# Context products on all 128 rows, bulk loads from ScalarE's queue, key scaling on GpSimd, one score bank per head

## The chip, the core and the metric

The kernel runs on one core of a Trainium2 chip. The core's engines run side by side and wait for each other by semaphores: TensorE (PE, with its weight loads shown apart as PEld), VectorE (DVE), ScalarE (ACT), GpSimd (POOL) and SyncE (SP), which here does nothing but issue DMAs. All DMAs run on the core's 16 DMA engines. The metric is device time of one execution, in microseconds (us).

## The reference, cut to what matters

The input is 4 sequences of 1024 tokens with 512 features. After a layer norm, an attention block and a small rounded product are added to the input. The attention has 16 heads of 128 features and two branches. The sparse branch attends to pooled entries (one for every four tokens, 256 a sequence), of which each query keeps the best 8. The local branch attends to a band of 128 tokens back. The two contexts are averaged and projected:

```python
q = apply_rope(rmsnorm(q, qn_w), pos)                       # 16 heads
ck = apply_rope(rmsnorm(entries @ Wk + bk, kn_w), block_ends)  # pooled keys, shared by the heads
cv = entries @ Wv + bv
sc = jnp.where(causal, einsum(q, ck) * scale, NEG)
tv, ti = jax.lax.top_k(sc, TOPK)                            # softmax over the best 8
lk = apply_rope(rmsnorm(hidden @ Wlk + blk, kn_w), pos)     # local keys, 16 heads
sl = jnp.where(band mask, q . lk * scale, NEG)              # 256 columns: last and this chunk
merged = (ctx_sparse + ctx_local) * 0.5
out = merged @ Wo + bo
```

`rmsnorm` divides by the root of the mean square and multiplies by a weight of the feature. `apply_rope` turns the first 64 features in pairs by an angle of the position: `x1*cos - x2*sin` and `x1*sin + x2*cos`.

## The kernel before

**Units and steps.** Tokens are cut into 32 chunks of 128, the heads into 8 pairs. One chunk with one pair of heads is a unit; there are 256. A step `s` of the main loop issues the scores of unit `s` and, in an order written out by hand, parts of the units around it: projections of unit `s+3`, normalization and rotation of `s+2`, values of `s+1`, context product of `s-1`, output projection of `s-2`. There is no scheduler's choice in it: each engine runs its instructions in the order of the text, and waits by semaphores where data or buffers are not ready.

**Chunks.** `c` is a chunk's place in its sequence, 0 to 7. It sets `m = 32 (c+1)`, the number of pooled entries that the unit's queries may see. The first 32 units (four chunks) run chunk by chunk. From unit `FIRST` = 32 on, units come in pairs of an even and an odd chunk, so `c` alternates (0, 1, 0, 1, ... for 16 units, then 2, 3, and so on), and the query and key projections of a pair are made together in seven products instead of eight, from combined weights: four blocks of 256 KB for each pair of heads, computed once by GpSimd, kept in DRAM and loaded again for each pair of chunks.

**The way of a unit.** `scores` (L964, L971, L974) writes both heads' scores to one PSUM tile of two banks. `weigh` adds masks and finds maxima on DVE (L995, L1009, L1016, L1017) and marks the best 8 (L1019); ACT then takes exponentials (L1021, L1029). `settle` on DVE drops what is not among the best 8 and takes the reciprocal of the sums (L1037, L1048); `divide` on ACT multiplies by it (L1055). `turn` transposes 32x32 blocks on DVE (L1073) and stores the result to DRAM (`pr<-probB`, L1081); `fetch` reads it back in four pieces with the blocks exchanged (`probT<-pr`, L1122), which makes a full transpose. `values` multiplies by the values (L1139) in the next step: for each head the last chunk's and this chunk's local values and one or two blocks of pooled values. Each such fp32 product appears as two MATMUL records. `keep_context` (L1155, ACT) and `to_output` (L1170, PE) end the unit.

**Queries and keys.** After the projection, ACT sums squares (`squares`, L413) and GpSimd makes the factor of each row and head (`spread`, L407 and L408). In the next step `normalize` multiplies on DVE by factor and weight, four instructions of 128x128 (L842), and `rotate` does the turn by angles: one product on GpSimd (L429), one on DVE (L431), sum and difference on GpSimd (L434, L435). `turn_keys` transposes blocks on DVE (L896, L899) and stores them (`qk<-thb`, L905, four DMAs); `fetch_keys` reads them back (L915, two).

**Queues.** From the first unit on, SyncE issues every load and store, in the order of the text. In a step of the pairs that order is: two of the pair's four loads of combined weights (`load_combined`, L352, 256 KB each, a ring of six places), `pr`, four `qk`, four `probT`, `qT` and `lkT`, stores of a chunk in preparation, and in every second step a load of output weights (`load_wo`, L169, 512 KB). Every DMA signals one of eight completion counters, taken in turn along the list of all DMAs, and in the built program a DMA waits at its issue until the DMA eight places before it has landed, unless that is known already. Across a step this ties `pr` and `qk` to pieces of the last `probT`.

The context product as it stands before:

```python
v, rows = cv[i - 2], min(P, m - P * (i - 2))
nc.tensor.matmul(blocks(cp[:, h, :]), v[0:rows],
    probT[0:rows, :, h * len(parts) + i - parts[0], :], ...)
```

Of the kernel before, what the change touches and what calls it, by code (L numbers as in the profile page):

```python
# [38 lines left out]
def kernel(  # L39
# [104 lines left out]
    wqk_sb = [const.tile([P, 2, 2, 2, 256], F32, name=f"wqk_{u}") for u in range(NU)]  # L144
# [3 lines left out]

    def row_of_weights(u, k):
        return wqk_sb[u][:, k // 2, :, k % 2, :]  # L150

    def load_wqk(u, engine):
        for i, w in enumerate((Wq, Wlk)):
            for j in range(2):
                engine.dma_start(
                    wqk_sb[u][:, j, i],
                    w[ts(j, 256), ts(u, 256)].rearrange("(k p) n -> p k n", p=P),
                )
# [24 lines left out]
    for k in range(KK):  # L183
        for i, w in enumerate((Wq, Wlk)):
            nc.sync.dma_start(wqk_sb[0][:, k // 2, i, k % 2, :], w[ts(k, P), 0:256])
# [109 lines left out]
    def fold_first_row(u):  # L295
        w = wqk_sb[u]
        row = first_row.pop(u, None)
        if row is None:

            row = pp(f"first_row_{u}")  # L300
            nc.tensor.matmul(
                row.rearrange("p (i n) -> p i n", i=2),
                ident[:, 0:1].to_broadcast([P, P]),
                row_of_weights(u, 0),
                start=True,
                stop=True,
            )
        row = row.rearrange("p (i n) -> p i n", i=2).unsqueeze(2)
        for j in range(2):
            nc.vector.tensor_tensor(  # L310
                w[:, j], w[:, j], row.to_broadcast([P, 2, 2, 256]), ALU.subtract
            )
        for i, bias in enumerate((bq, blk)):
            nc.sync.dma_start(
                w[0:1, 0, i, 0, :], bias[ts(u, 256)].partition_broadcast(1)
            )

    combined = [
        dram.tile([4, P, 512], F32, tag=f"combined_{u}", name=f"combined_{u}", bufs=1)
# [6 lines left out]
    def combine_weights():  # L326

        one, two = (v.rearrange("p h d -> p (h d)") for v in th_tiles[2:])
        for u in range(NU):
            (b11, b12), (b21, b22) = (  # L330
                [flat(wqk_sb[u][:, j, i]) for i in range(2)] for j in range(2)
            )
            for i, (to, a, b) in enumerate(
                ((one, b12, b11), (two, b22, one), (one, b21, two), (two, b22, b12))
            ):
                nc.gpsimd.tensor_tensor(to, a, b, ALU.subtract)
                stores.append((combined[u][(0, 1, 3, 2)[i]], to))
                yield

    places = [flat(wqk_sb[u][:, 0, 1]) for u in range(NU)]  # L340
    ring = places[0:4] + places[6:8]
    token_sums = [
        v.rearrange("p (k s) -> p k s", k=2)
        for at in places[4:6]
        for v in (at[:, 0:256], at[:, 256:512])
    ]
    loaded = {}

    def load_combined(q, which):
        for i in which:  # L350
            at = ring[(4 * (q - FIRST // 2) + (2, 0, 1, 3)[i]) % len(ring)]
            nc.sync.dma_start(at, combined[q % NU][i])  # L352
            loaded[q, i] = at.rearrange("p (k n) -> p k n", k=2)
# [408 lines left out]
    def p1(q):  # L762
        p, u = divmod(q, NU)
        xa, one = chunks[2 * p]
        product(0, (one, xa[:, 1, :]), wqk_sb[u][:, 0, 0])
# [5 lines left out]
    def p2(q):  # L771
        p, u = divmod(q, NU)
        product(1, both(chunks[2 * p][0][:, 2:4, :]), wqk_sb[u][:, 1, 0])

    def p6(q):
        product(0, both(token_sums[1]), loaded.pop((q, 1)), False)
# [5 lines left out]
    def p7(q):  # L782
        product(2, both(token_sums[2]), loaded.pop((q, 2)))

    def p5(q):
        product(0, both(token_sums[0]), loaded.pop((q, 0)), False)
# [4 lines left out]
    def p3(q):  # L791
        _, u = divmod(q, NU)
        product(0, both(token_sums[3]), wqk_sb[u][:, 1, 1], False)
# [4 lines left out]
    def p4(q):  # L798
        p, _ = divmod(q, NU)
        product(2, both(chunks[2 * p + 1][0][:, 2:4, :]), loaded.pop((q, 3)), False)  # L800
# [35 lines left out]
    def normalize(n):  # L836
        w = units[n]
        r = w["r"]
        src = sources(n)
        th = pools["th"].take(n) if "qp" in w else w["th"]  # L840
        for i in range(4):
            nc.vector.scalar_tensor_tensor(  # L842
                th[:, i, :],
                src[i],
                r[:, i : i + 1],
                norm_w[:, i // 2, :],
                ALU.mult,
                ALU.mult,
            )
        thb = work.tile([P, NB, 2, 2 * BLK], F32, tag="thb", name=f"thb_{n}", bufs=1)  # L850
        spare = thb.rearrange("p b t x -> p (b t x)")[:, 0 : 4 * ROPE]
        w["rotation"] = rotate(th, angles[place(n)[0]], 4, spare, f"{n}")
        next(w["rotation"])
        w["th"], w["thb"] = th, thb

# [91 lines left out]
    def scores(n, h):  # L947
# [6 lines left out]
        if n == NN - 2:  # L954

            w.setdefault("sc", []).append(qk_banks[h])
        elif not h:
            sc = psum.tile([P, 2, 512], F32, tag="sc", name=f"sc_{n}", bufs=1)
            w["sc"] = [sc[:, 0, :], sc[:, 1, :]]
            w["sc_both"] = sc  # L960
# [17 lines left out]
    def weigh(n):  # L978
# [5 lines left out]
            work.tile([P, 1], F32, tag=f"neg_{h}", name=f"neg_{h}_{n}") for h in range(2)  # L984
        ]
        neg_spa = work.tile([P, 2, 1], F32, tag="neg_spa", name=f"neg_spa_{n}")
        tot = work.tile([P, 2, 2], F32, tag="tot", name=f"tot_{n}")
        taken = work.tile([P, 2, 2 * P], BF16, tag="taken", name=f"taken_{n}", bufs=1)
        if n == 0:

            for prob in probs:
                nc.gpsimd.memset(prob[:, 2 * P + NE : 4 * P], 0.0)

        for h in range(2):
            nc.vector.tensor_tensor_reduce(  # L995
                sc[h][:, loc],
                sc[h][:, loc],
                mask_b[:, loc],
                -1.0,
                TAKEN,  # L1000
                ALU.add,
                ALU.min,
                neg[h],
            )
        newest = ds(2 * P + m - NE, NE)
        mask = mask_b[:, 2 * P : 2 * P + NE]
        if "sc_both" in w:
            last = w.pop("sc_both")[:, :, newest]
            nc.vector.tensor_tensor(  # L1009
                last, last, mask.unsqueeze(1).to_broadcast([P, 2, NE]), ALU.add  # L1010
            )
        else:
            for h in range(2):
                nc.vector.tensor_tensor(sc[h][:, newest], sc[h][:, newest], mask, ALU.add)
        for h in range(2):
            nc.vector.max(top[:, h, :], sc[h][:, spa])  # L1016
        nc.vector.tensor_scalar(neg_spa, top[:, :, 0:1], -1.0, 1e29, ALU.mult, ALU.min)  # L1017
        for h in range(2):
            nc.vector.match_replace(taken[:, h, 0:m], top[:, h, :], sc[h][:, spa], TAKEN)  # L1019
        for h in range(2):  # L1020
# [4 lines left out]
                bias=neg[h],  # L1025
# [3 lines left out]
            nc.scalar.activation(probs[h][:, spa], sc[h][:, spa], AF.Exp, bias=neg_spa[:, h, :])  # L1029
# [54 lines left out]
    def turn_here(n):  # L1084
# [4 lines left out]
        if n >= NN - 2:  # L1089
            banks = qk_banks  # L1090
        elif n == NN - 3:
            both = psum.tile([P, 2, 512], F32, tag="sc", name=f"tp_{n}", bufs=1)
            banks = [both[:, 0, :], both[:, 1, :]]
        else:
            banks = [pp(f"tp_{n}_{h}") for h in range(2 if g > 2 else 1)]
# [31 lines left out]
    def values(n):  # L1127
        _, m, _, _ = columns(n)
# [4 lines left out]
        for h in range(2):  # L1133
            for i in parts:
                if i < 2:
                    v, rows = (w if i else units[before(n)])["lv"][:, h, :], P
                else:
                    v, rows = cv[i - 2], min(P, m - P * (i - 2))
                nc.tensor.matmul(  # L1139
                    blocks(cp[:, h, :]),  # L1140
                    v[0:rows],
                    probT[0:rows, :, h * len(parts) + i - parts[0], :],
# [114 lines left out]
    for s in range(-3, NN - 3):  # L1257
# [17 lines left out]
        if odd:  # L1275
            for_pair(q, (p5,), (keep5,))
# [7 lines left out]
        if even:  # L1284
            for_pair(q + 1, (load_combined, (1, 2)))
        else:
            for_pair(q + 1, (load_combined, (0, 3)))
# [10 lines left out]
        for_unit(s + 2, (normalize,))  # L1298
        if s == FIRST - 4:
            for_pair(q, (p1,), (keep1,), (p2,))  # L1300
        for_unit(s - 2, (to_output,))
        if even:
# [8 lines left out]
        for_unit(s + 2, (go_on_rotating,), (end_rotation,))  # L1311
# [3 lines left out]
        if odd:  # L1315
            for_pair(q, (p3,), (keep3,))
        if by_dma(s):
            turn(s)
        if s + 2 >= NU:
# [5 lines left out]
        for_unit(s + 3, (squares, (0, 1, 2, 3)), (spread,))  # L1325
        steps()
# [29 lines left out]
        elif s > FIRST and odd:  # L1356
            load_wo(s + 1, nc.sync)
# [20 lines left out]
        if s in angles_at:  # L1378
            load_angles(angles_at[s])
        if s > 0 and before(s - 1) is not None:  # L1380
# [9 lines left out]
    normalize(c)  # L1390
    settle(a)
    divide(a)
    go_on_rotating(c)
    end_rotation(c)
# [79 lines left out]
```

## Time and profile before

| | |
|---|---|
| time, median of 3 runs | 2914.75 us (2910.6 to 2928.78) |
| the profiled execution | 2914.57 us, of which its span 2912.7 us |
| granted TensorE clock | 0.966 |
| PE, PEld busy | 2718.6 us (93%), 2132.2 us (73%) |
| DVE, ACT, POOL busy | 2160.6, 1567.3, 1076.2 us (74, 54, 37%) |
| DMA engines busy | 74% of the span by SyncE's queue |

The page of a profile gives busy time by engine, then the chain of work that ended last (followed back from the end, at each step to what released the step), then groups of instructions: line, engine, operation, what it writes from what, shape, how many, and behind the bar the busy time in us and the mean of one in ns. A view of waits gives, for an engine and a line, whom it waited for: us in total, how often, the longest. Instructions of one engine overlap a little, so a row's mean is longer than the distance of two starts. Where the text speaks of distances between instructions of one unit, they are taken from the same trace's start and end times, over units 40 to 249.

### The profile page before, as it was taken

To read this page: it belongs to the slowest core of one execution; us is meant where nothing else is said; L and a number is where in the kernel's file an instruction comes from. 1 tells how busy PE (TensorE), PEld (TensorE's weight loads), DVE (VectorE), ACT (ScalarE), POOL (GpSimd) and SP (SyncE) were. 2 spreads that over 40 slices of the span, in tenths; PEclk is the share of its full clock that TensorE was granted. 3 is DMA by queue.
4 is the path that set the end of the run, shared out by engine and by line. 5 is a ranking of instruction groups with operands and counts; after the bars stand their busy time and mean duration, and the time that the engine had idled before them with its cause. 6 is when DMAs were issued, how large, how long until landed. Compare 5 with 4: busy or idle time off the path is not lost.

```text
span 2912.7 us, 50814 instructions
## 1 busy us (share of the span) xinstructions
PE 2718.6 (93%) x13170; PEld 2132.2 (73%) x13205; DVE 2160.6 (74%) x7725; ACT 1567.3 (54%) x6000; POOL 1076.2 (37%) x1714
## 2 busy tenths in 40 slices
PE   8998889998999999999999998999999999899998
PEld 5665567777777777777777777777777777777876
DVE  6777668787876877778776777777877768676776
ACT  3444455555555655556555555555555556555555
POOL 5455433332333333333333433333333333332332
PEclk9999999999999999999999999999999999999999
DMA  7477777787777777778777677777777667777874
GB/s 241 117 218 223 223 227 218 217 236 209 213 206 210 222 205 210 214 211 231 223 211 206 202 223 205 211 223 218 233 220 214 197 205 218 217 226 217 232 218 134
DMA packets 825490, 619.18 MB, mean 213 GB/s; under 512 B 402911, under 2 KB 678512, under 8 KB 825200
## 3 DMA queue, kind: packets, MB, share of 16 engines
q1 hardware_dynamic: 825168, 615.91, 74.0%
q8 instruction: 107, 1.75, 0.3%
q14 instruction: 183, 1.50, 0.2%
q10 hardware_dynamic: 32, 0.02, 0.0%
HBM read 414.08 MB, written 201.59 MB: 211 GB/s over the span
## 4 chain that ended last, share of the span: by engine, by line
PE 51%; DMA 20%; DVE 13%; ACT 6%; SPq 6%; issue 3%; POOL 0%; ACTq 0%; DVEq 0%; POOLq 0%
PE vc L1139 13%; PE qk L744 12%; DMA pr<-probB 12%; DMA probT<-pr 7%; PE out L1170 7%; PE vc L922 6%; SPq L1122 4%; PE sc L974 3%; PE sc L971 3%; ACT prob L1055 3%; PE sc L964 3%; DVE sc L995 2%; PE pp L744 2%; DVE prob L1037 2%; DVE taken L1019 1%
## 5 line engine op out<-in xcount | busy, mean ns | idle before, releaser
L995 DVE CUSTOM_DVE_ANT_0 sc<-sc,mask_b 128x256 f32<-128x256 f32 (+1 forms) x510 | 211.7, 415 | 498.5 <-PE sc L974 489.3
L429 POOL TENSOR_TENSOR rb<-th,cs 128x256 f32<-128x256 f32 x256 | 194.1, 758 | 955.0 <-DVE th L842 954.9
L1055 ACT ACTIVATE prob<-prob,tot 128x256 f32<-128x256 f32 (+7 forms) x1024 | 381.9, 443 | 221.6 <-DVE tot L1048 221.3
L1170 PE MATMUL out<-wo,cT 128*128 128x512 f32 x1024 | 486.2, 597 | 12.4 <-DMA wo<-in_L_attn_Wo_dram 7.8
L922 PE MATMUL vc<-wlv,tokens 128*128 128x256 f32 x2048 | 487.5, 381 | 4.3 <-ACT lv L934 4.3
L1139 PE MATMUL vc<-probT,lv 128*128 128x128 f32 x1920 | 335.8, 297 | 155.7 <-DMA probT<-pr 152.9
L922 PEld LDWEIGHTS vc<-wlv,tokens 128*128 128x128 f32 x2048 | 391.7, 191 | 120.8 <-issue 69.6
L744 PE MATMUL qk<-wqk,wqk 128*128 128x256 f32 x1736 | 457.8, 387 | 0.0
L1021 ACT ACTIVATE prob<-sc,neg 128x256 f32<-128x256 f32 (+1 forms) x510 | 234.9, 461 | 399.2 <-DVE taken L1019 395.4
L1139 PEld LDWEIGHTS vc<-probT,lv 128*128 128x128 f32 x1920 | 277.0, 199 | 224.8 <-issue 151.1
L744 PEld LDWEIGHTS qk<-wqk,wqk 128*128 128x128 f32 x1736 | 319.0, 192 | 90.1 <-issue 48.5
L1073 DVE STREAM_TRANSPOSE probB<-prob 128x512 f32<-128x512 f32 (+2 forms) x490 | 308.8, 632 | 100.2 <-ACT prob L1055 77.7
L1170 PEld LDWEIGHTS out<-wo,cT 128*128 128x128 f32 x1024 | 193.8, 191 | 162.4 <-issue 136.3
L1139 PE MATMUL vc<-probT,cv 128*128 128x128 f32 (+3 forms) x1536 | 309.6, 304 | 0.0
L413 ACT ACTIVATE junk<-th 128x128 bf16<-128x128 f32 x896 | 275.1, 307 | 21.2
L408 POOL TENSOR_TENSOR r<-r,nhalf 128x4 f32<-128x4 f32 x256 | 273.7, 1069 | 21.4
L744 PE MATMUL qk<-wqk,tokens 128*128 128x256 f32 x896 | 263.0, 420 | 0.2 <-DVE th L842 0.2
L1139 PEld LDWEIGHTS vc<-probT,cv 128*128 128x128 f32 (+3 forms) x1536 | 234.7, 200 | 32.7 <-issue 4.0
L842 DVE SCALAR_TENSOR_TENSOR th<-th,r,norm_w 128x128 f32<-128x128 f32 x896 | 255.8, 348 | 0.0
L1037 DVE SCALAR_TENSOR_TENSOR prob<-taken,prob 128x96 f32<-128x96 bf16 (+7 forms) x512 | 233.3, 464 | 19.1 <-ACT prob L1029 10.8
L974 PE MATMUL sc<-ckT,qT 128*128 128x160 f32 (+5 forms) x1020 | 231.2, 309 | 0.0
L434 POOL TENSOR_TENSOR th<-thb,rb 128x128 f32<-128x128 f32 x256 | 117.1, 457 | 304.2 <-DVE thb L431 297.9
(206 smaller groups left out, 4542.2 us busy)
## 6 DMA issues: line engine op xcount, KB each, us to landing
wqk<-combined SPq DMA_DIRECT2D x448, 256.0 KB
wo<-in_L_attn_Wo_dram SPq DMA_DIRECT2D x144, 512.0 KB
pr<-probB SPq DMA_DIRECT2D x125, 512.0 KB
probT<-pr SPq DMA_DIRECT2D x500, 128.0 KB
qk<-thb SPq DMA_DIRECT2D x992, 64.0 KB
pr<-probB SPq DMA_DIRECT2D x96, 384.0 KB
probT<-pr SPq DMA_DIRECT2D x384, 96.0 KB
qT<-qk SPq DMA_DIRECT2D x248, 128.0 KB
```

The source lines that it names most:

```text
L408: nc.gpsimd.tensor_tensor(r, r, nhalf[: ss.shape[0], 0:n], ALU.pow)
L413: nc.scalar.activation(junk[: src.shape[0]], src, AF.Square, accum_out=acc)
L744: nc.tensor.matmul(regions[i], a[k], b[:, k, :], start=first and k == 0, stop=k == 1, skip_group_check=not first,)
L842: nc.vector.scalar_tensor_tensor(th[:, i, :], src[i], r[:, i : i + 1], norm_w[:, i // 2, :], ALU.mult, ALU.mult,)
L922: nc.tensor.matmul(vp, xnT[:, k, :], wlv_sb[u][:, k, :], start=(k == 0), stop=(k == KK - 1),)
L974: nc.tensor.matmul(sc[:, spa], q, ckT[:, 0:m], start=True, stop=True)
L995: nc.vector.tensor_tensor_reduce(sc[h][:, loc], sc[h][:, loc], mask_b[:, loc], -1.0, TAKEN, ALU.add, ALU.min, neg[h],)
L1037: nc.vector.scalar_tensor_tensor(probs[h][:, spa], taken[:, h, 0:m], TAKEN_FROM, probs[h][:, spa], ALU.is_ge, ALU.mult, accum_out=tot[:, h ...
L1055: nc.scalar.mul(probs[h][:, cols], probs[h][:, cols], tot[:, h, part : part + 1])
L1073: nc.vector.transpose(pb[:, :, ds(h * g, g), :], prob[:, parts[0] * P : (parts[-1] + 1) * P].rearrange("p (g b i) -> p b g i", b=NB, i=BLK),)
L1139: nc.tensor.matmul(blocks(cp[:, h, :]), v[0:rows], probT[0:rows, :, h * len(parts) + i - parts[0], :], start=(i == parts[0]), stop=(i == p ...
L1170: nc.tensor.matmul(op, cT[:, h, :], wo[:, h, :], start=(u == 0 and h == 0), stop=(u == NU - 1 and h == 1),)
```

## The change

- `values` uses all 128 rows of the pooled values and of `probT` in every product. Columns of `prob` past `m` are set to zero by GpSimd where they can be read: all of them at the start of a sequence, 32 columns in each even unit from `FIRST` on.
- The combined weights lie in DRAM and SBUF so that a pair needs two loads of 512 KB, not four of 256 KB. They are issued by ScalarE, one in each step, right after `keep_context`; there are two places, one for each load. From `FIRST` on, the load of output weights is issued by ScalarE too, behind the exponentials of every second step.
- From `FIRST` on, GpSimd multiplies each head by its factor (four instructions) and makes the sine product, both in the step before; DVE then makes one product of 128x512 with a table of weight times cosine, and GpSimd adds and subtracts as before. The tables of weight times cosine and weight times sine are made by GpSimd once a chunk. `turn_keys` stands before `turn` instead of behind it.
- Each head's scores have a PSUM tile of their own; in `weigh` all of DVE's work on head 0 and its exponentials stand before those of head 1. The mask of the newest 32 columns and the sign of the sparse maximum, one instruction for both heads before, become one for each.

```diff
+    def load_combined(q, g):
+        nc.scalar.dma_start(places[g], combined[q % NU][g].rearrange("p e (k n) -> p e k n", k=2))
...
+    def make_tables(t):
+        cs = angles[t]
+        for lo, at in ((0, 0), (HALF, D)):
+            nc.gpsimd.tensor_tensor(
+                tables[t % 2][:, :, at : at + ROPE].rearrange("p g (t f) -> p g t f", t=2),
+                norm_w[:, :, 0:ROPE].rearrange("p g (t f) -> p g t f", t=2),
+                cs[:, lo : lo + HALF].unsqueeze(1).unsqueeze(1).to_broadcast([P, 2, 2, HALF]),
+                ALU.mult,
+            )
...
+    def scale_and_turn(n):
+        w = units[n]
+        th, r = w["th"], w["r"]
+        for i in range(4):
+            nc.gpsimd.tensor_scalar(th[:, i, :], th[:, i, :], r[:, i : i + 1], None, ALU.mult)
+        w["rb"] = work.tile([P, 4 * ROPE], F32, tag="ropeb", name=f"rb_{n}", bufs=1)
+        nc.gpsimd.tensor_tensor(
+            w["rb"].rearrange("p (g h d) -> p g h d", g=2, h=2),
+            th[:, :, 0:ROPE].rearrange("p (g h) d -> p g h d", g=2),
+            tables[place(n)[0] % 2][:, :, D:].unsqueeze(2).to_broadcast([P, 2, 2, ROPE]),
+            ALU.mult,
+        )
+
+    def rotate_all(n):
...
+        nc.vector.tensor_tensor(
+            v,
+            v,
+            tables[place(n)[0] % 2][:, :, 0:D].unsqueeze(2).to_broadcast([P, 2, 2, D]),
+            ALU.mult,
+        )
...
+        nc.gpsimd.tensor_tensor(x12[:, :, 0, :], x12[:, :, 0, :], bb[:, :, 1, :], ALU.subtract)
+        nc.gpsimd.tensor_tensor(x12[:, :, 1, :], x12[:, :, 1, :], bb[:, :, 0, :], ALU.add)
...
-        elif not h:
-            sc = psum.tile([P, 2, 512], F32, tag="sc", name=f"sc_{n}", bufs=1)
-            w["sc"] = [sc[:, 0, :], sc[:, 1, :]]
-            w["sc_both"] = sc
+        else:
+            sc = psum.tile([P, 512], F32, tag=f"sc_{h}", name=f"sc_{h}_{n}", bufs=1)
+            w.setdefault("sc", []).append(sc)
...
+        elif n >= FIRST and n % 2 == 0:
+            for prob in probs:
+                nc.gpsimd.memset(prob[:, 2 * P + m : 2 * P + m + NE], 0.0)
...
-                    v, rows = cv[i - 2], min(P, m - P * (i - 2))
+                    v = cv[i - 2]
...
-                    v[0:rows],
-                    probT[0:rows, :, h * len(parts) + i - parts[0], :],
+                    v,
+                    probT[:, :, h * len(parts) + i - parts[0], :],
...
         if odd:
+            for_pair(q + 1, (load_combined, 0))
+        else:
+            for_pair(q, (load_combined, 1))
+        if odd:
             for_pair(q, (p5,), (keep5,))
...
-        if even:
-            for_pair(q + 1, (load_combined, (1, 2)))
-        else:
-            for_pair(q + 1, (load_combined, (0, 3)))
...
-        for_unit(s + 2, (normalize,))
+        old = s + 2 < FIRST
+        for_unit(s + 2, (normalize,) if old else (rotate_all,))
...
+        if s > FIRST and odd:
+            load_wo(s + 1, nc.scalar)
...
+        if s + 2 >= FIRST:
+            for_unit(s + 2, (turn_keys,))
         if by_dma(s):
             turn(s)
-        if s + 2 >= NU:
+        if NU <= s + 2 < FIRST:
             for_unit(s + 2, (turn_keys,))
...
         for_unit(s + 3, (squares, (0, 1, 2, 3)), (spread,))
+        if s + 3 >= FIRST:
+            for_unit(s + 3, (scale_and_turn,))
...
-        elif s > FIRST and odd:
-            load_wo(s + 1, nc.sync)
```

## The prediction

> **What bounds the kernel now.** I read the busy line first, then the chain that ended last.
>
> ```profile
> PE 2718.6 (93%) x13170; PEld 2132.2 (73%) x13205; DVE 2160.6 (74%) x7725; ACT 1567.3 (54%) x6000; POOL 1076.2 (37%) x1714
> ...
> PE 51%; DMA 20%; DVE 13%; ACT 6%; SPq 6%; issue 3%; POOL 0%; ACTq 0%; DVEq 0%; POOLq 0%
> PE vc L1139 13%; PE qk L744 12%; DMA pr<-probB 12%; DMA probT<-pr 7%; PE out L1170 7%; PE vc L922 6%; SPq L1122 4%; PE sc L974 3%; PE sc L971 3%; ACT prob L1055 3%; PE sc L964 3%; DVE sc L995 2%; PE pp L744 2%; DVE prob L1037 2%; DVE taken L1019 1%
> ```
>
> TensorE has little slack, yet only half of the last chain is its work. A fifth is two transfers, `pr` and `probT`, the transposition of the probabilities through DRAM. The view of waits names what TensorE lacks, and its SyncE part where that path stands:
>
> ```profile
> PE vc L1139 <- DMA probT<-pr: 152.9, 98, 5.3
> ```
>
> ```profile
> SPq L1122 <- DMA pr<-probB: 255.3, 189, 4.1
> SPq L1081 <- DVE probB L1073: 208.6, 83, 7.6
> ```
>
> So nearly all of TensorE's idle time is one wait, for `probT`. Counted over the records of units 40 to 249, a step takes 11.14 us, of which TensorE idles 0.66; even units wait (100 us in 57 places) more than odd ones (32 us in 25). The chain in time shows why, at an even unit:
>
> ```profile
> 1508.49 0.29 SPq L1341
> ...
> 1510.17 0.63 SPq L1341
> ...
> 1510.84 0.62 SPq L169
> ...
> 1511.50 0.48 SPq L352
> ...
> 1513.03 4.97 DMA pr<-probB
> ...
> 1519.37 2.09 DMA probT<-pr
> ...
> 1521.60 1.70 PE vc L1139 x8
> ```
>
> `pr` was ready at 1510.2, when DVE's transposes end, but SyncE was still issuing stores (L1341), output weights (L169) and combined weights (L352). Then `pr` took 4.97 us behind their data. Where TensorE waited for an even unit, `pr` to its landing took 5.0 us; where it did not, 3.6.
>
> The loop is: scores of a unit, its probabilities, `pr`, `probT`, values in the next step; two steps last as long as this way plus the values and some 0.9 us to the scores after. The mean way from scores to values is 19.2 us, and 19.2 + 2.15 + 0.9 is 22.3, twice 11.14. Both limits lie close together: TensorE's own work in two steps is 20.0, 19.8, 22.3 and 21.3 us for c = 0/1, 2/3, 4/5, 6/7.
>
> **Part 1: all rows.** The groups with shapes apart:
>
> ```profile
> L1139 PE MATMUL vc<-probT,cv 128*128 128x128 f32 x768 | 144.4, 285 | 0.0
> ...
> L1139 PE MATMUL vc<-probT,cv 32*128 32x128 f32 x256 | 67.0, 344 | 0.0
> L1139 PE MATMUL vc<-probT,cv 64*128 64x128 f32 x256 | 62.8, 325 | 0.0
> ```
>
> Fewer rows are not cheaper. The whole stage, at its shortest, lasts 2.52, 2.53, 1.95 and 1.95 us for c = 4, 5, 6, 7, and 1.63, 2.08, 1.50, 1.50 for c = 0 to 3: 96 rows cost as much as 128, 32 and 64 rows cost 0.57 us more, in gaps at the change of shape. The first product behind takes 0.48 us instead of 0.38. I take 0.65 us a unit (0.57 to 0.75), in half of the 256 units: **-83 us** (-73 to -96), all on TensorE and in the loop as well. The zeroing on GpSimd is two small instructions in every second step (192 ns is the smallest GpSimd row here), while it idles.
>
> **Part 2: DVE, ScalarE and GpSimd.**
>
> ```profile
> L842 DVE SCALAR_TENSOR_TENSOR th<-th,r,norm_w 128x128 f32<-128x128 f32 x896 | 255.8, 348 | 0.0
> ...
> L431 DVE TENSOR_TENSOR thb<-th,cs 128x256 f32<-128x256 f32 x256 | 108.8, 425 | 22.4 <-DMA qk<-thb 20.9 <-DMA lkT<-qk 0.7 <-DMA qT<-qk 0.3
> ...
> L407 POOL TENSOR_SCALAR r<-ss 128x4 f32<-128x4 f32 x256 | 58.6, 229 | 423.8 <-ACT junk L413 419.7
> ...
> L519 DVE TENSOR_TENSOR x<-xb,row 128x512 f32<-128x512 f32 x31 | 21.7, 701 | 1.0
> ...
> L380 POOL TENSOR_SCALAR qm_x<-qv_x 128x512 f32<-128x512 f32 x32 | 19.9, 622 | 0.1
> ```
>
> DVE loses four L842 (1.13 us by their starts) and L431, and gets one product of 128x512 (0.70, as L519). The score banks let head 0's exponentials start 1 us sooner, but head 1's work now runs as a second dependent row of five, with two small instructions more: +0.35 us before the last maximum is marked. `settle` stands behind the 128x512 product on DVE: 0.35 - 0.43 is -0.08 us, nothing. The earlier exponentials are not what it waits for.
>
> A GpSimd scaling of 128x128 isn't shown; it lies between 0.23 (128x4) and 0.62 (128x512). I take 0.33, by the elements between the two, so 1.3 us for four and 0.76 for the sine product. DVE needs them 0.75 us after the place where it now marks the maxima. The room from the factor's end to there is 3.1 us in the median even step and 2.3 in the lower quarter, against 2.1. That fits at 0.33; at 0.62 (3.2 us) it is late in half of the even steps. GpSimd goes from 4.2 to about 5.5 us a step.
>
> [...]
>
> **Part 3: the queues.** ScalarE issues three DMAs in two steps at 0.28 to 0.58 us (its two issues at the start). The loads stand before copies that idle for TensorE (L789 and L769, 235 and 185 us in 224 steps), the output weights in the pause before `divide` (L1055 waits 221 us, 237 times): hidden.
>
> SyncE loses 1.1 us of issuing a step (two L352 and half an L169), but now issues `qk` before `pr`. Four `qk` issues take 1.81 us undisturbed. From the reciprocal: transposes 0.76, issue 1.81, so `pr` at 2.6 us (odd) or 2.95 (even, one DVE addition in between); before, 2.79 and 2.96 in the mean. No gain, less spread. `pr` to landing: 3.69 (odd) and 4.36 (even) before; without output weights ahead and with one 512 KB load beside, I take 3.25, between the shortest seen (2.6) and 4.4. [...]
>
> The loop of a unit is then: scores to reciprocal (5.9, 6.4, 6.7, 6.8, 7.4, 7.3, 7.8, 8.0 us for c = 0 to 7, as before), 5.85 (odd) or 6.2 (even) to the landing of `pr`, 4.4 to the values (the median where TensorE waited), values at 128 rows (1.06, three times 1.5, four times 1.95), 0.9 to the next scores. The longer of each pair is 19.0, 19.6, 20.8 and 21.2 us in two steps; TensorE's work is 18.7, 19.8, 21.0, 21.3. Made for the kernel before, the same sum lies 0.6 to 1.0 us under the measured two steps, by stores and preparations. I add 0.6 to the larger of the two limits: idle 0.9, 0.6, 0.6, 0.6 in two steps, 0.35 a step, 224 x 0.35 = 78 us in place of 0.66 x 221 = 146. **-68 us** (-146 if no wait is left; +30 if the landings stay and SyncE's new order costs 0.4 a step).
>
> **Part 4: new waits between the queues.** By the built program's wait lists, a DMA waits for the one eight places before it. In 29 steps (places 0, 7 and 12 of a block of 16 steps) a `qk` piece, and once `pr`, waits for a combined load that ScalarE issues in the next step, behind `keep_context`. SyncE stands, with `pr` and `probT` behind it. That load is issued when the next step's scores start and lands 2.8 us later; `pr` goes at +3.4 instead of -0.1, and lands some 0.5 faster alone: 3.0 us late, 2.7 beyond what is idle anyway. 30 x 2.7 = 81. In 14 of these a `probT` piece also waits for the next step's output weights, 1.0 us more: 14. In 51 steps a `qk` piece waits for the same step's output weights, 0 to 1.2 us, by the piece: 10. **+105 us** (15 if loads land at once or the loop has slack, 205 if a load needs 5.0 us, as `pr` did when crowded).
>
> **The sum**, on the profiled 2914.6 us (span 2912.7 and 1.9 around it; the median of the runs is 2914.75): -83 - 68 + 105 = -46, so **2868 us**.
>
> **Rivals.** (A) *The loop falls below TensorE.* For it: waits sit where output weights and stores crowded SyncE. Then -130 instead of -68, and the stalls of part 4 are partly slack, +65: 2914.6 - 83 - 130 + 65 = 2767; I call this case all below 2840. (B) *The split gives nothing:* landings as before, part 3 at 0: 2914.6 - 83 + 105 = 2937. For it: the DMA engines are busy 74% either way. GpSimd late by 0.3 us a step (67 us on the forecast) ends at the same place, 2935. (C) *Slower: SyncE held by ScalarE.* Loads that land in 5.0 us hold `pr` 5.2 us late in 30 places (156), and output weights hold pieces 1.2 us in 40 (49): 205, with part 3 at -25: 2914.6 - 83 - 25 + 205 = 3012. It decides from 2944 on, where this part costs 137 us: 24 for the output weights and 3.8 us a place. Against it: SyncE's halt leaves the DMA engines empty for the very load.
>
> **How the numbers follow.** The forecast (2840 to 2885) has 0.34, A 0.22, B (2886 to 2943) 0.22, C 0.22. One per cent, 29 us, is about what a measurement of this kernel can tell from no change. Faster by over 1%: 0.34 + 0.22 = 0.56; within: 0.22; slower: 0.22. The range reaches from A's middle to well into C: 2770 to 2975.
>
> **What would show it.** Right: all L1139 groups at 128 rows near 285 ns; the new DVE product near 0.70 and GpSimd's scalings near 0.33 us; TensorE's wait for `probT` gathered in few long pieces of 3 us, with SyncE waiting for `wqk` or `wo` before `qk`; otherwise `pr` landing in 3 to 3.5 us. Wrong: no long SyncE waits for ScalarE's loads (then A); DVE waiting for GpSimd before its new product; TensorE's wait for `probT` spread over most units (B).

## The result, and the profile after

The changed kernel takes 3166 us in the median (3148 to 3172) where the kernel before takes 2913 on the same chip. By the means of the runs (3162 and 2916) that is a ratio of 1.084, 95% interval 1.079 to 1.089. The forecast was 2868 (2770 to 2975). The profiled execution took 3148.3 us, span 3146.6. The page after: busy times, the granted clock over the span, and the chain that ended last by engine and by line.

```profile
PE 2707.0 (86%) x13205; PEld 2158.0 (69%) x13205; DVE 2064.3 (66%) x7340; ACT 1579.9 (50%) x6000; POOL 1655.7 (53%) x2892
...
PEclk9999998998899989899999989999999999899999
...
PE 42%; DMA 32%; DVE 9%; SPq 7%; issue 4%; POOL 4%; ACT 2%; ACTq 0%; DVEq 0%; POOLq 0%
PE vc L1190 13%; DMA probT<-pr 12%; DMA pr<-probB 12%; PE qk L767 10%; PE out L1221 5%; SPq L1174 5%; PE vc L975 4%; DMA wqk<-combined 3%; PE sc L1026 2%; PE sc L1023 2%; DMA lkT<-qk 2%; PE sc L1016 2%; DMA wo<-in_L_attn_Wo_dram 2%; POOL th L884 2%; ACT prob L1105 1%
```

Transfers rose from 20% to 32% of the chain, and among the lines shown stand three transfers that did not before: combined weights, `lkT` and output weights. The mean granted clock fell from 0.966 to 0.934; its row, all nines before, has eights in it now. TensorE still lacks `probT`:

```profile
PE vc L1190 <- DMA probT<-pr: 368.8, 135, 8.1
...
DVE th L897 <- POOL rb L886: 74.5, 82, 2.8
```

That wait was 152.9 us, 98 times. SyncE's part of the view of waits names why:

```profile
SPq L1174 <- DMA pr<-probB: 694.0, 242, 5.9
SPq L958 <- DVE thb L952: 212.3, 86, 6.2
SPq L958 <- DMA wqk<-combined: 128.5, 38, 5.9
SPq L958 <- DMA wo<-in_L_attn_Wo_dram: 82.1, 40, 5.9
SPq L968 <- DMA wqk<-combined: 66.8, 44, 4.8
SPq L610 <- DMA wo<-in_L_attn_Wo_dram: 36.9, 14, 4.1
```

SyncE stores keys (L958), fetches them (L968) and fetches tokens (L610), and waits there for loads that ScalarE issued: 356 us with the smaller rows of this kind. The timeline shows one such place whole:

```profile
1545.63 0.45 ACTq L176 DMA_DIRECT2D wo<-in_L_attn_Wo_dram  x1
...
1548.10 0.40 DVE L952 STREAM_TRANSPOSE thb<-th 128x256 f32<-128x256 f32 x1
1548.64 1.51 DVE L1123 STREAM_TRANSPOSE probB<-prob 128x512 f32<-128x512 f32 x2
...
1551.80 1.77 SPq L958 DMA_DIRECT2D qk<-thb  x4
1553.67 0.39 SPq L1131 DMA_DIRECT2D pr<-probB  x1
```

and SyncE's waits from 1540 to 1570 us name what held the first key store:

```profile
SPq L958 <- DMA wo<-in_L_attn_Wo_dram: 4.2, 1, 4.2
```

The keys lie ready at 1548.5 and the scores at 1550.15. The first of the four key stores goes at 1551.8, when the output weights issued 6.2 us earlier have landed, and `pr` leaves behind the fourth, 3.5 us after it was ready.

The groups with shapes apart:

```profile
L884 POOL TENSOR_SCALAR th<-th,r 128x128 f32<-128x128 f32 x896 | 526.9, 605 | 22.3
L1190 PE MATMUL vc<-probT,lv 128*128 128x128 f32 x1920 | 363.6, 317 | 382.9 <-DMA probT<-pr 368.8 <-issue 4.6 <-DMA qk<-thb 4.4
L1190 PE MATMUL vc<-probT,cv 128*128 128x128 f32 x1536 | 300.2, 312 | 0.0
L897 DVE TENSOR_TENSOR th<-th,wqk 128x512 f32<-128x512 f32 x224 | 204.6, 913 | 76.2 <-POOL rb L886 74.5
```

The scaling costs 605 ns, not 330, the new product 913 in the mean, not 700, and the products at 128 rows 312 to 317, not 285. Counted over the records of units 40 to 249 as before, a step takes 12.18 us instead of 11.14, and TensorE idles 1.72 us of it instead of 0.66.

### The profile page after: what moved, and what is told of

It reads as the page before. It is cut to its first block, busy times and chain, and to the rows that moved or that the text cites. A ratio compares the mean times of both kernels' runs of the same rounds, so it can differ in the third digit from the quotient of the medians.

```text
span 3146.6 us, 50946 instructions
## 1 busy us (share of the span) xinstructions
PE 2707.0 (86%) x13205; PEld 2158.0 (69%) x13205; DVE 2064.3 (66%) x7340; ACT 1579.9 (50%) x6000; POOL 1655.7 (53%) x2892
## 4 chain that ended last, share of the span: by engine, by line
PE 42%; DMA 32%; DVE 9%; SPq 7%; issue 4%; POOL 4%; ACT 2%; ACTq 0%; DVEq 0%; POOLq 0%
PE vc L1190 13%; DMA probT<-pr 12%; DMA pr<-probB 12%; PE qk L767 10%; PE out L1221 5%; SPq L1174 5%; PE vc L975 4%; DMA wqk<-combined 3%; PE sc L1026 2%; PE sc L1023 2%; DMA lkT<-qk 2%; PE sc L1016 2%; DMA wo<-in_L_attn_Wo_dram 2%; POOL th L884 2%; ACT prob L1105 1%
## 5 line engine op out<-in xcount | busy, mean ns | idle before, releaser
L1190 PEld LDWEIGHTS vc<-probT,lv 128*128 128x128 f32 x1920 | 307.8, 223 | 449.0 <-issue 337.7
L884 POOL TENSOR_SCALAR th<-th,r 128x128 f32<-128x128 f32 x896 | 526.9, 605 | 22.3
L767 PE MATMUL qk<-wqk 128*128 128x256 f32 x1792 | 485.9, 396 | 9.5 <-POOL wqk L383 9.5
L430 POOL TENSOR_SCALAR r<-ss 128x4 f32<-128x4 f32 x256 | 53.0, 207 | 688.6 <-ACT junk L436 684.7
L767 PEld LDWEIGHTS qk<-wqk 128*128 128x128 f32 x1792 | 342.9, 200 | 99.6 <-issue 43.5
L905 POOL TENSOR_TENSOR th<-th,rb 128x128 f32<-128x128 f32 x224 | 109.7, 490 | 451.3 <-DVE th L897 441.4
L1190 PE MATMUL vc<-probT,cv 128*128 128x128 f32 x1536 | 300.2, 312 | 0.0
L1190 PEld LDWEIGHTS vc<-probT,cv 128*128 128x128 f32 x1536 | 256.5, 227 | 0.0
L897 DVE TENSOR_TENSOR th<-th,wqk 128x512 f32<-128x512 f32 x224 | 204.6, 913 | 76.2 <-POOL rb L886 74.5
L987 ACT COPY lv<-vc 128x256 f32<-128x256 f32 x256 | 93.3, 365 | 311.0 <-PE vc L1190 307.5
```

What stands on the lines that cost most here:

```text
L767: nc.tensor.matmul(regions[i], a[k], b[:, k, :], start=first and k == 0, stop=k == 1, skip_group_check=not first,)
L884: nc.gpsimd.tensor_scalar(th[:, i, :], th[:, i, :], r[:, i : i + 1], None, ALU.mult)
L897: nc.vector.tensor_tensor(v, v, tables[place(n)[0] % 2][:, :, 0:D].unsqueeze(2).to_broadcast([P, 2, 2, D]), ALU.mult,)
L1190: nc.tensor.matmul(blocks(cp[:, h, :]), v, probT[:, :, h * len(parts) + i - parts[0], :], start=(i == parts[0]), stop=(i == parts[-1]),)
```

## The experiments

All ratios are to the kernel before, on the same chip, with 95% intervals. Two times with a stroke between them are means over even and over odd units among 40 to 249, counted over the records. The trace of the kernel before is from the first comparison, where that kernel took 2913 us; beside the experiments it took 2900 to 2902, some 0.05 us a step less.

### Single parts undone

Loads by SyncE (the output weights at their place of before, the combined weights still two of 512 KB):

```diff
-        nc.scalar.dma_start(places[g], combined[q % NU][g]...
+        nc.sync.dma_start(places[g], combined[q % NU][g]...
-        if s > FIRST and odd:
-            load_wo(s + 1, nc.scalar)
...
+        elif s > FIRST and odd:
+            load_wo(s + 1, nc.sync)
```

> The changed kernel with one part undone: the combined loads (still two of 512 KB per pair of units) and the output weights' loads are issued by SyncE again, the output weights at the end of the step as before the change. The changed kernel stands at 1.084 of the kernel before (3166 us). Theory Q (SyncE stands still on loads that ScalarE issued: about 339 us of its waits end with such a load): those waits go, the score fetch is issued earlier, and the time falls by 150 to 250 us, to a ratio of 1.00 to 1.035. Theory G (GpSimd's scaling at 605 ns a row group and the 913 ns product are what is late): the time stays above 1.06. Theory K (order of keys and scores on SyncE): it stays above 1.06 too.

Measured: 3013.5 us, 1.038 (1.032 to 1.043). All SyncE waits on these loads are gone. Just above what theory Q expected: 4.7 points of the changed kernel's 8.4 hang on the queue, but not all.

Normalisation and rotation on VectorE (the keys still first):

```diff
-        for_unit(s + 2, (normalize,) if old else (rotate_all,))
+        for_unit(s + 2, (normalize,))
...
-            for_unit(s + 3, (scale_and_turn,))
```

> The changed kernel with one part undone: normalisation and rotation of all units are VectorE's four products and the rotation as before the change; no tables, no scaling on GpSimd. The keys still go ahead of the scores on SyncE. Theory G: GpSimd's 527 us of scaling leave the path, matching to settling returns from 1.54 to 1.38 us and the weighing-to-reciprocal chain from 5.60 to 5.29 us, and the waits on GpSimd (74 us at the product) go: down by 70 to 150 us, ratio 1.03 to 1.06. Theory Q: VectorE gets 0.4 us a step longer in front of the turning of the keys, which only adds to the delay: within 20 us of the changed kernel, ratio 1.075 to 1.095.

Measured: 3313.7 us, 1.143 (1.137 to 1.148). Both theories missed: 5.8 points slower. From the reciprocal to the keys' last transpose the time grew from 1.13 to 2.4 us and to the end of the scores' transposes from 2.5 to 3.4, since VectorE now rotates the keys in between; `pr` is issued 6.06/5.84 us after the reciprocal instead of 5.38/5.62. The granted clock is lower too (0.913 for 0.934). With the keys first, GpSimd's part is a help.

Scores ahead of the keys:

```diff
-        if s + 2 >= FIRST:
-            for_unit(s + 2, (turn_keys,))
         if by_dma(s):
             turn(s)
-        if NU <= s + 2 < FIRST:
+        if s + 2 >= NU:
             for_unit(s + 2, (turn_keys,))
```

> The changed kernel with one part undone: in the rotated units too the scores are turned, and stored by SyncE, ahead of the keys, as before the change. Theory K (the keys' four stores, and what they wait for, stand before the scores' store): the time from the reciprocal to the issue of the scores' store falls from a median of 4.4 to 5.4 us back to about 2.6, and the time by 100 to 200 us, ratio 1.015 to 1.05. Theory Q: the waits on ScalarE's loads fall on the next instruction in the queue, the score store or fetch, instead: the time falls by less than 60 us, ratio above 1.06. Theory G: no change, 1.08.

Measured: 3015.9 us, 1.039 (1.034 to 1.043), as theory K had it. Reciprocal to the issue of `pr`: 5.38/5.62 to 2.87/2.96 us. SyncE still waits 390 us for ScalarE's loads, but now with the scores' store already gone.

### Two and three parts undone

> The changed kernel with two parts undone at once, each of which alone brought it from 1.084 to 1.038: the loads are SyncE's again, and the scores are stored ahead of the keys. Left of the change: all rows, the scaling on GpSimd with the product, the score banks, the loads of 512 KB. If the two costs are separate and add up (theory Q+K): 1.084 - 0.047 - 0.046, a ratio of 0.98 to 1.00. If both are one cost seen twice (the SyncE queue is late once, by either): 1.02 to 1.04. Theory G (GpSimd is what is left): above 1.00 in either case, with settling on every even step with chunk work at 2 us and more behind the matching.

Measured (the first and third edit together): 2940.8 us, 1.012 (1.008 to 1.017). Neither expectation was met: together the two edits take away 7.2 points where their single gains make 9.3. So there are two costs, not one seen twice, but each is larger beside the other. What is left above 1 is GpSimd's and the layout's. VectorE's wait in it:

```profile
DVE th L897 <- POOL rb L886: 190.2, 140, 4.1
```

Settling comes 2.50 us after matching on even units, against 1.43 in the next run, where only GpSimd's part is taken out too; on odd units it is late in both (2.53 and 2.47).

> The changed kernel with three parts undone: loads by SyncE, scores ahead of keys, normalisation on VectorE. Left: all rows, the score banks, loads of 512 KB. All rows alone gave 0.991. If GpSimd's scaling still costs something where the order is right (theory G), this is faster than the run with two parts undone by 0.01 to 0.03: ratio 0.975 to 0.99. If the scaling on GpSimd is a gain for VectorE (as in the changed kernel, where taking it back cost 5.4%), this is slower than that run by 0.005 or more. The price of banks and 512 KB loads together is its distance to 0.991; the prediction had it at nothing.

Measured (all three edits): 2905.0 us, 1.000 (0.997 to 1.003). GpSimd's part costs 1.2 points where the order is right, as much as theory G said, though the ratio misses its 0.975 to 0.99. What is left (rows, banks, two places of 512 KB) is still no gain; TensorE has a new wait:

```profile
PE qk L767 <- DMA wqk<-combined: 145.7, 69, 4.5
```

> The changed kernel with the scores ahead of the keys and normalisation on VectorE; the loads of 512 KB and the output weights' loads stay ScalarE's. Set beside the run that differs from it in the loads' queue alone, this prices ScalarE's queue in the order of the kernel before. Theory Q (SyncE stands still on ScalarE's loads, about 280 us of it in the run with the scores first): slower than that run by 0.02 to 0.05, a ratio of 1.00 to 1.04. The prediction's part 3 alone (68 us of shorter landings and no costs): faster by 0.02, ratio 0.96 to 0.98.

Measured (second and third edit): 2985.5 us, 1.028 (1.022 to 1.034). Beside the run before it, ScalarE's queue costs 2.8 points; SyncE's waits on its loads are 394 us in all. The longest such row:

```profile
SPq L958 <- DMA wqk<-combined: 111.6, 31, 6.0
```

### Single parts on the kernel before

All rows:

```diff
-                    v, rows = cv[i - 2], min(P, m - P * (i - 2))
+                    v = cv[i - 2]
...
-                    v[0:rows],
-                    probT[0:rows, :, h * len(parts) + i - parts[0], :],
+                    v,
+                    probT[:, :, h * len(parts) + i - parts[0], :],
```

> The kernel before with one part of the change alone: the products of context over all 128 rows, with the zeros that the cut rows then need (two 124 ns memsets by GpSimd on every even step). The prediction's first part: 0.65 us off half of the 256 values stages, 83 us, where TensorE's idle of 0.66 us a step stays: ratio 0.967 to 0.975 (2819 to 2842 us). Its rival (the saved time turns into waiting, since the scores come back no earlier): ratio 0.99 to 1.00.

Measured: 2874.4 us, 0.991 (0.987 to 0.994): within the rival's range, a third of what the prediction gave. The groups and the wait:

```profile
L1141 PE MATMUL vc<-probT,lv 128*128 128x128 f32 x1920 | 327.7, 293 | 215.7 <-DMA probT<-pr 211.4 <-issue 3.6 <-ACT probT L1114 0.5
L1141 PE MATMUL vc<-probT,cv 128*128 128x128 f32 x1536 | 271.5, 288 | 0.0
```

TensorE's own work in a step falls from 10.48 to 10.06 us, more than the 0.33 expected, but its idle time rises from 0.66 to 0.91. The way from scores to values stays 19.2 us. Only the stage of values in the loop is shorter, by 0.27 in the mean, and that loop lasts two steps: a step gains 0.17, of which some 0.05 is the other chip's, so about half of 0.27.

A bank per head, and weighing head by head (that hunk of the change's diff alone):

> The kernel before with one part of the change alone: a score bank for each head, and weighing head by head with two maskings of the newest entries and two negations where there was one of each. The prediction: +0.35 us before the second maximum, -0.43 us from the shorter start, so nothing: ratio 0.995 to 1.005. Its rival: the two more VectorE instructions of 0.15 to 0.2 us a step stand in front of matching, whose end moves from 2.64 to 2.99 us after the start of weighing in the changed kernel: 0.35 x 250 = 88 us where it is all on the path, ratio up to 1.03.

Measured: 2873.5 us, 0.989 (0.985 to 0.992): a gain that neither side expected. Weighing to reciprocal is 0.29 us longer (5.29 to 5.58), but weighing starts 1.04 us after the scores instead of 1.79, and scores to values falls from 19.22 to 18.87. VectorE's wait for scores, before and in this run:

```profile
DVE sc L995 <- PE sc L974: 489.3, 213, 10.1
```

```profile
DVE sc L999 <- PE sc L973: 361.2, 197, 8.9
```

The expectation misread the prediction: its -0.43 us is what VectorE saves by the scaling on GpSimd (1.13 less 0.70), so for the banks alone the prediction's sum gave +0.35, a loss.

Both together:

> The kernel before with the two parts that gain alone, all rows (0.991) and the score banks (0.989), with its own loads, queues, order and normalisation. If the gains add: 0.975 to 0.985 (about 2845 us). If both shorten the same loop and TensorE is then the bound: 0.985 to 0.992.

Measured: 2866.8 us, 0.987 (0.984 to 0.990), the best of all runs. They hardly add. TensorE still idles 0.86 us a step, so it is not yet the bound that the second expectation named.

The keys first, on the kernel before:

> The kernel before with one part of the change alone: the keys of the rotated units are turned and stored ahead of the scores. Theory K, by the four runs that differ in this order alone or nearly (1.084 to 1.039 with ScalarE's loads, 1.038 to 1.012 with SyncE's): the time from the reciprocal to the issue of the scores' store grows from 2.9 to over 4 us, ratio 1.02 to 1.04. With VectorE's rotation, which ends later than GpSimd's, more: 1.03 to 1.06 (taking the scaling back to VectorE with the keys first cost 1.084 to 1.143). The prediction (it gains nothing and loses nothing, with less spread): 0.99 to 1.01.

Measured: 3086.1 us, 1.064 (1.060 to 1.068), just above theory K's range, though no load is ScalarE's. Reciprocal to `pr`: 2.96/2.79 to 5.49/5.01. SyncE's longest wait in this run, and a stretch of its timeline:

```profile
SPq L1122 <- DMA pr<-probB: 667.2, 242, 5.0
```

```profile
1509.03 0.42 SPq L169 DMA_DIRECT2D wo<-in_L_attn_Wo_dram  x1
...
1510.00 0.92 SPq L352 DMA_DIRECT2D wqk<-combined  x2
1511.02 1.81 SPq L905 DMA_DIRECT2D qk<-thb  x4
1512.97 0.47 SPq L1081 DMA_DIRECT2D pr<-probB  x1
1516.90 1.73 SPq L1122 DMA_DIRECT2D probT<-pr  x4
```

The four stores come on top of the loads that already stood ahead of `pr`. And SyncE then stands 667 us (before: 255) for `pr` to land, since the key stores no longer fill that time.

### What in the queue costs, and what in the layout

The loads by GpSimd (otherwise the run with ScalarE's queue and scores first):

```diff
-        nc.scalar.dma_start(places[g], combined[q % NU][g]...
+        nc.gpsimd.dma_start(places[g], combined[q % NU][g]...
```

> As the run with scores first, normalisation on VectorE and the loads on ScalarE's queue (ratio 1.028), but the 512 KB loads and the output weights' loads are issued by GpSimd. In the built program ScalarE's DMAs and SyncE's take the same eight completion counters in turn (301 DMAs of SyncE's wait for one of ScalarE's); GpSimd's DMAs have counters of their own, and none of SyncE's waits for one. Same loads, same places, no waits between the queues. Theory Q (the shared counters are what ScalarE's queue costs): SyncE's waits on combined and output weights, 345 us in that run, are gone, and the ratio falls by 0.025 or more, to 0.98 to 1.00. If it is the loads' data in the way of the scores' transfers: the ratio stays within 0.01 of 1.028. GpSimd's own issue cost may add to either.

Measured: 2907.9 us, 1.000 (0.998 to 1.003) instead of 1.028. No wait on one of these loads is left in SyncE's list, which begins:

```profile
SPq L1131 <- DVE probB L1123: 337.4, 125, 7.8
...
SPq L1174 <- DMA pr<-probB: 178.9, 182, 3.3
```

In the changed kernel's trace the 336 DMAs of ScalarE and the 3443 of SyncE signal the same eight completion counters. So what ScalarE's queue costs is SyncE's waits on its loads (394 us in the run at 1.028, none here), not the loads' data. The data are in the way as well, but with either second queue alike. A DMA's landing can be read from the trace as the last update of its completion counter before the counter's next DMA:

| loads of 512 KB from | `pr` lands after | last of four `probT` pieces, after the fetch begins | ratio |
|---|---|---|---|
| SyncE | 4.37 us | 4.30 us | 1.000 |
| ScalarE | 3.33 us | 5.80 us | 1.028 |
| GpSimd | 3.39 us | 5.93 us | 1.000 |

What `pr` gains, `probT` loses. Either second queue also takes away TensorE's wait of 146 us for combined weights, and with GpSimd's the ratio is 1.000 all the same: a queue of its own brings these loads nothing.

A third place, so that each load is issued a step earlier; first on ScalarE's queue, then on SyncE's:

```diff
+    ring = [places[0], places[1], places[3]]
...
+        at = ring[(2 * (q - FIRST // 2) + g) % 3]
...
+        for_pair(q + 1, (load_combined, odd))
```

> As the run with scores first, normalisation on VectorE and the loads on ScalarE's queue (ratio 1.028), with a third place of 512 KB, so that each load is issued a step earlier than its use needs and never waits for a place. The waits between the counters are the same (SyncE's DMAs that wait for one of ScalarE's, by line: 89, 63, 78 and so on, as in that run). Theory Q: SyncE's waits on the loads stay at 250 to 350 us and the ratio stays at 1.015 to 1.035. If ScalarE's waiting for a free place is what makes the loads late: it falls to 0.98 to 1.00.

Measured: 2981.5 us, 1.029 (1.024 to 1.033); SyncE's waits on the loads 392 us. An earlier issue does not help, as theory Q said.

> As the run with all rows, score banks and 512 KB loads on SyncE (ratio 1.000), with a third place for the loads. There TensorE waited 146 us (69 times) for combined weights, where the kernel before has six places of 256 KB and its loads a step ahead. If the two places are the price of that layout: these waits go, and the ratio falls to 0.975 to 0.99. If large loads in front of the scores' transfers are its price: it stays at 0.995 to 1.005.

Measured: 2918.0 us, 1.006 (1.003 to 1.008). The wait for combined weights is gone, yet nothing is gained: `pr` to the next fetch takes 5.13/4.64 us where the kernel with four loads of 256 KB takes 4.68/3.97.

Each of these loads as two of 256 KB:

```diff
+        for e in range(2):
+            nc.sync.dma_start(at[:, e], combined[q % NU][g][:, e]...
```

> As the run with the third place and 512 KB loads on SyncE (ratio 1.0055), with each load issued as two of 256 KB to the same place, as many and as large as in the kernel before. There the scores' transfer took 5.13 us on even and 4.64 us on odd units from its issue to the next fetch, and 4.68 and 3.97 with the loads of the kernel before (ratio 0.987). If the size of one load is what delays the scores: the ratio returns to 0.985 to 0.993 and these times to 4.7 and 4.0. If it is something else in the layout: 1.00 to 1.01.

Measured: 2897.4 us, 0.999 (0.997 to 1.001), and 4.80/4.15 us. The size of a load explains the landing times nearly, and 0.7 of the 1.8 points; the rest of the layout's price stays open.

GpSimd's queue for the kernel with rows and banks:

> The kernel before with all rows and the score banks (0.987), and its own four loads of 256 KB and the output weights' loads issued by GpSimd, whose DMAs share no counter with SyncE's. With 512 KB loads the move from SyncE (1.000) to GpSimd left the time as it was. If SyncE's issue time (1.1 us a step) ahead of the scores' store still costs: 0.975 to 0.985. If not, or if more waiting of GpSimd takes its place: 0.985 to 1.00.

Measured: 2956.1 us, 1.020 (1.017 to 1.024), slower than expected by either side. `pr` lands sooner (3.88/3.05), but from the fetch to the values it takes 6.44/7.31 instead of 4.53/5.34. Here too the last `probT` piece lands later (6.02 us after the fetch begins instead of 4.23), and this kernel had no wait for combined weights to lose by the move. Whether that is all that makes 256 KB loads dear there and 512 KB loads not was not tried.

## Why the prediction was wrong

Read from the kernel with rows and banks upwards, one part at a time, the runs make a ladder that ends at the change:

| kernel | ratio | step on 2914.6 us |
|---|---|---|
| rows and banks, own loads, queues and order | 0.987 | -37 |
| + 512 KB layout with two places | 1.000 | +37 |
| + GpSimd's scaling and the product | 1.012 | +36 |
| + ScalarE's queue | 1.039 | +76 |
| + keys ahead of scores (the change) | 1.084 | +133 |

Each step is the difference of two ratios times 2914.6; single ones are good to about 20 us. Taken in another order the last two are +73 for the keys and +136 for the queue: each costs more beside the other.

**Part 1 (all rows, -83): mis-sized, -27 alone.** The price of the cut rows was about right (0.27 us off the stage in the mean for 0.33); the step that failed is "all on TensorE and in the loop as well". TensorE did not set the pace, the loop did, and a unit's stage stands in it once in two steps. Where the loop binds, half the saving counts. The saving in TensorE's work was there (0.42 us a step), but more than half of it came back as idle time.

**Part 2 (nothing): two errors of opposite sign, whose sum is near nothing by luck.** The scaling is 0.60 us, the upper bound and not the 0.33 taken. The consequence that the prediction gave for 0.62, lateness in half of the even steps, is what came (VectorE waits in 61 of 112 even steps and 21 odd ones; with loads by SyncE and the scores first in 90 and 50), and costs 36 us in the right order. The banks gain 33 us alone: the +0.35 us was about right (0.29), but the sum left out that head 0's own weighing starts before head 1's scores are done, 0.75 us sooner.

**Part 3 (-68): failed, and the largest error.** The landing of `pr` was right (3.38/3.71 to the next fetch for 3.25). The issue was not: 2.95 and 2.6 us from the reciprocal were forecast, 5.38 and 5.62 came. "Four `qk` issues take 1.81 us undisturbed" holds, but the sum had SyncE free when the keys are turned. In the changed kernel the last key transpose ends 1.1 us after the reciprocal, the first store goes 1.5 to 2.0 us later, and `pr` 2.5 to 2.7 us after that. Even with no ScalarE load `pr` goes at 4.61/3.93: the first store goes 1.0 to 1.5 us after the last key transpose, behind earlier loads and stores. And the fetch's standing time that the stores used to fill went uncounted. "No gain, less spread" was worth 133 us the wrong way. The other failed term is the 4.4 us to the values, kept as before: what takes loads out of `pr`'s way puts them into that of `probT`, whose last piece lands 5.05 us after the fetch begins instead of 4.23 (5.8 with the scores first). The upper bound, +30 us for an order that costs 0.4 us a step, was too small by its own figures: 0.4 x 224 is 90. The order cost 0.33 us a step with SyncE's loads and 0.6 with ScalarE's.

**Part 4 (+105): right in mechanism and about right in size**, 76 with the scores first, 136 with the keys first. A term inside it was mis-sized: the sum had a load of 512 KB land in 2.8 us, and the shortest in the traces of before and after took 3.4. By the counters the output weights took 4.5 us in the median before (3.7 at the least), and in the changed kernel 4.4, the combined loads 4.3; those shown in the timeline took 6.2. So the same step's output weights, which were to hold `qk` pieces for 10 us in all, held SyncE at the key stores for 82 (40 waits, the longest 5.9).

**The layout (no term): +37**, through loads that TensorE or the scores' transfer waits for, as far as the runs tell.

The rival that came nearest, C, had the right sign and one of the causes, but at 3012 too little: none of the rivals charged the new order of SyncE; only part 3's upper bound did. B's late GpSimd is real at half its price (36 for 67 us), and A's slack is nowhere to be seen.

As to the signs named: long waits of SyncE before `qk` are there, `pr` lands in 3.4 to 3.7 us, VectorE waits for GpSimd 82 times. The 285 ns at 128 rows came true only with rows alone (288).

A second issuing engine gave the loads of 512 KB nothing in these runs: from GpSimd's queue, with no SyncE wait on them, 1.000, from SyncE's 1.000, and what `pr` gains (3.39 us to its landing for 4.37) `probT` loses (5.93 for 4.30). The four loads of 256 KB were slower on a second queue (1.020 against 0.987).

## What to carry to other kernels

Before a step is moved ahead of another on an in-order queue, count its issue time, all that stands ahead of it then, and the waiting time that it used to fill; here that was half the loss. Moving DMAs to a second issuing engine did not free the first of them here: ScalarE's loads signal the eight counters that SyncE's DMAs signal too, and SyncE waited 356 us for them. Read the built program's wait lists. And a saving in a stage counts by how often the stage stands in the loop that binds: find that loop before the saving is multiplied by the number of steps.

## What the runs showed of the hardware

**Beside a GpSimd product the new VectorE product took up to 2.5 times as long.** The new 128x512 product has one instruction and one shape, but 681 to 1744 ns. In the 119 executions with GpSimd idle the median is 685 ns. Beside a GpSimd product of two tensors (68 executions) it is up to 1.74 us, as in this stretch of the changed kernel's timeline:

```profile
1480.88 1.27 POOL L700 TENSOR_TENSOR x<-x,bo_sb 128x512 f32<-128x512 f32 x1
1480.96 1.74 DVE L897 TENSOR_TENSOR th<-th,wqk 128x512 f32<-128x512 f32 x1 [0.67 <-POOL rb L886]
```

Beside GpSimd's memsets alone it stays at 692 ns (36 executions). GpSimd's scaling, with one tensor and a factor per partition, takes 602 ns in the median whether VectorE works or not.

**Behind waits of 3 to 5 us TensorE's values products took 421 ns, not 275.** The trace's record of the granted clock has two values, 1 and 0.5. It stands at 0.5 for 414 us in the changed kernel, in 77 spells of mostly 3.4 or 6.8 us, and for 199 us in the kernel before. Of TensorE's 59 waits over 3 us after the change, 56 have such a spell begin in them or within 3.5 us behind them. In the changed kernel, values products within 2.5 us after a wait of 3 to 5 us take 421 ns in the median, after one below 1 us 275, and later than 6 us after any wait 275. The waits over 3 us number 13 in the kernel before (95 in the run at 1.143, granted clock 0.913). TensorE's work in a step is 10.46 us at clock 0.934 in the changed kernel and 10.06 at 0.971 with all rows alone, and 10.06 x 0.971 / 0.934 is 10.46. So I estimate that 0.4 us a step, some 90 us in 224, of the change's loss came through the clock, which hid the gain of all rows.
